# Attention in a fused block: divisions in whole steps, narrow diagonal steps unsummed, the bias earlier, another order at the end

## The chip, the cores and the metric

The kernel runs on one core of one Trainium2 chip. The time is the device time of one execution in microseconds; the figure compared is the median of several runs. The core's engines work side by side, each on its own queue: TensorE (PE, with its weight loads listed as PEld), VectorE (DVE), ScalarE (ACT), GpSimd (POOL) and SyncE (SP, which here issues the transfers).

## What is computed

A block of a transformer on 2048 tokens of width 512: half a feed-forward layer, causal attention with 16 heads of 32, half a feed-forward layer again, each on a layer norm and each added to the residual.

```python
x = x + 0.5 * _L0_ffn_ref(_layernorm(x, axis=-1), ...)
x = x + _L0_attn_ref(_layernorm(x, axis=-1), ...)
x = x + 0.5 * _L0_ffn_ref(_layernorm(x, axis=-1), ...)

# _L0_attn_ref
qkv = jnp.einsum('bsd,ed->bse', x, w_qkv) + b_qkv
...
scores = jnp.einsum('bhqd,bhkd->bhqk', q, k) / math.sqrt(Hd)
causal = jnp.triu(jnp.full((S, S), -jnp.inf, dtype=scores.dtype), k=1)
attn = jax.nn.softmax(scores + causal[None, None], axis=-1)
out = jnp.einsum('bhqk,bhkd->bhqd', attn, v)
...
return jnp.einsum('bsd,ed->bse', out, w_out) + b_out
```

All is float32. The feed-forward layers also unpack 4-bit weights; the change does not touch them.

## The kernel before

The program is one hand-ordered stream: the order in which the Python code calls the operations is the order of each engine's queue. Three stages follow each other: the first feed-forward layer, attention, the second feed-forward layer.

Attention takes the heads two at a time, in eight pairs `p`. Within a pair the 2048 queries are four blocks `g` of 512. `attend` walks over the key tiles (128 keys each) of a block, in an order in which the four tiles on the diagonal stand last (blocks 0 to 2) or in the middle (block 3). So a pair has 4 + 8 + 12 + 16 = 40 steps. In one step PE makes the scores of one key tile for both heads of the pair (lines 1323 and 1332, transposed: keys in the partitions, queries along the free axis), ACT takes the exponential into a tile `pt` (line 1357), and two steps later PE multiplies it with the values (line 1255). In the diagonal steps only the queries from the offset `off` on (0, 128, 256 or 384) are alive; the 128x128 corner of one head is masked by DVE on the scores, that of the other by ACT's copy (1350), a select on POOL (1351) and ACT's exponential (1359). In the same steps PE and DVE work ahead: `maxima(p + 1)` makes the scores of the next pair once more the other way round (line 1183), and DVE takes their largest values (1191, 1195), which come back as a negative row through `split` (1201 to 1220) and are added to the scores by PE in line 1323. Pair 0's maxima are made before any `attend`, in a loop of 40 steps.

The softmax denominators come from PE too: a matmul of line 1255 with a tile of ones in place of the values. To halve their number, two neighbouring steps' exponentials are first added up (`add`, lines 1378 and 1380): by POOL in pairs 0 to 6, by DVE in pair 7. If the second step's offset is larger, the first step's remaining columns are copied (line 1378). The sum of a diagonal pair is made at the end of the step after it. Only the last two steps of block 3 are left unsummed, with two matmuls in place of one. `columns` puts the 512 queries of two heads into four groups of 32 output partitions: the even and odd 128-query parts of each head.

At the end of a block, ACT copies numerators and denominators out of the bank (`both`, line 1277). In pairs 0 to 6 the denominators go through memory into a packed form, are inverted there (line 1289, four steps later), and come back spread out as `rc`; from the eighth step on, POOL multiplies (`chunk`, line 1301), one 32x128 piece for each head and each 128 queries, two at a step. Pair 7 inverts directly (line 1298). `at` sets the step at which such a piece is put into the stream.

After every second pair, `project_out` multiplies the finished 128 rows with the output weights and DVE adds the result to the residual tiles `xs` (line 1139); pair 7's share is in `o2` and `o3`. The output bias is added to `xs` by POOL in the first 16 steps of pair 0 (line 1487). The scores, maxima and projections share seven PSUM banks (`ps_one`).

At the end of attention stand: the transposed, normed tokens `xT_f` for the second feed-forward layer; sums of their blocks (`outer_sums`, `inner_first`); the last values matmuls; pair 7's last divisions; and 12 output projections. The second feed-forward layer begins by sending residual tiles 8 to 15 to memory (line 657), on SP's queue ahead of the weight loads, and with further sums on DVE (lines 695 and after).

Of the kernel before, what the change touches and what calls it, by code (L numbers as in the profile page):

```python
# [10 lines left out]
F32 = mybir.dt.float32  # L11
# [5 lines left out]
ALU = mybir.AluOpType  # L17
AX = mybir.AxisListType

P = 128  # L20
# [3 lines left out]
HD = 32  # L24
NT = S // P
NB = S // 512
NG = 8
NPAIR = H // 2
# [7 lines left out]
def macaron_kernel(ctx: ExitStack, tc: tile.TileContext, x, packed, scales, wqk, bqk, wv, bv, wo, bo, out):  # L36
# [6 lines left out]
    nc = tc.nc  # L43
# [18 lines left out]
    xs = [xpair[t // 2][:, t % 2, :] for t in range(NT)]  # L62
# [978 lines left out]
    def attention(xT, xT_f, wqk_wv, next_w):  # L1041
        with tc.tile_pool(name="aw", bufs=1) as aw, tc.tile_pool(name="qk", bufs=1) as qkp, tc.tile_pool(
            name="pp", bufs=4
# [87 lines left out]
            def project_out(u):  # L1131


                def piece(t):
                    po = ps_one.tile([P, 512], F32, tag="one", name=f"pp_{u}_{t}")
                    nc.tensor.matmul(  # L1136
                        po, lhsT=attnT[u][:, bass.ts(t, P)], rhs=wo_sb[:, u, :], start=True, stop=True
                    )
                    nc.vector.tensor_tensor(xs[t], po, xs[t], ALU.add)

                return [lambda t=t: piece(t) for t in range(NT)]

            def quadrant(p, a):
                r = 2 * (p % 2) + a
                return slice(HD * r, HD * r + HD)
# [4 lines left out]
            def at(steps, piece):  # L1150
                divisions.setdefault(now + steps, []).append(piece)
# [77 lines left out]
            def attend(p, width):  # L1229
# [7 lines left out]
                def order(g):  # L1237
                    return around(g, list(range(4 * g)), list(range(4 * g, 4 * g + 4)))
# [27 lines left out]
                def values(g, n, off, pt):  # L1266
                    c = order(g)[n]
                    if n == 0:

                        avs[0] = ps_acc.tile([P, 2, 256], F32, tag="acc", name=f"av_{p}_{g}")  # L1270
                    columns(0, pt, off, v=vals[:, c, p % 4, :], start=(n == 0))
                    last = n + 1 == len(order(g))
                    if (n > 0 and n % 2 == 0) or last:
                        denominators()
                    if last:
                        both = an.tile([P, 2, 256], F32, tag="both", name=f"both_{p}_{g}")
                        nc.scalar.copy(both, avs[0])  # L1277
                        rc = dens[g % 2]
                        direct = p == NPAIR - 1
                        if not direct:  # L1280

                            flat = store.tile([4, 256], F32, tag=f"flat{g % 2}", name=f"flat_{p}_{g}")
                            packs = an.tile([16, 64], F32, tag="packs", name=f"packs_{p}_{g}")
                            for r in range(4):
                                nc.sync.dma_start(out=flat[r : r + 1, :], in_=both[HD * r : HD * r + 1, 1, :])
                            nc.sync.dma_start(out=packs, in_=flat.rearrange("a (j n) -> (a j) n", j=4))

                        def inverse():
                            nc.vector.reciprocal(packs, packs)
                            back = store.tile([4, 256], F32, tag=f"back{g % 2}", name=f"back_{p}_{g}")  # L1290
                            nc.sync.dma_start(out=back.rearrange("a (j n) -> (a j) n", j=4), in_=packs)
                            for r in range(4):
                                nc.sync.dma_start(out=rc[HD * r : HD * r + HD, :], in_=back[r].partition_broadcast(HD))

                        def chunk(j):
                            n = slice(j // 2 * P, j // 2 * P + P)
                            if direct and j % 2 == 0:
                                nc.vector.reciprocal(rc[:, n], both[:, 1, n])
                            for a in range(2):
                                r = slice(HD * (2 * a + j % 2), HD * (2 * a + j % 2) + HD)  # L1300
                                nc.gpsimd.tensor_tensor(
                                    dst[quadrant(p, a), bass.ts(4 * g + j, P)], both[r, 0, n], rc[r, n], ALU.mult
                                )

                        if not direct:
                            at(4, inverse)
                        for j in range(4):
                            at((2 if direct else 8) + j, lambda j=j: chunk(j))

                def step(g, n, copied):  # L1310
                    c = order(g)[n]
# [51 lines left out]
                    def tail():  # L1363
                        while summing:
                            summing.pop(0)()
                        if n % 2 == 1:
                            (one, off_1), (other, off_2) = two
                            two.clear()
                            if g + 1 == NB and n + 1 == len(order(g)):

                                summed.append([(one, off_1), (other, off_2)])
                            else:
                                s = pp.tile([P, 2, 512], F32, tag="sum", name=f"sum_{p}_{g}_{n}", bufs=2)
                                eng = nc.vector if p + 1 == NPAIR else nc.gpsimd

                                def add():
                                    if off_1 < off_2:
                                        eng.tensor_copy(s[:, :, off_1:off_2], one[:, :, off_1:off_2])
                                    for a in range(2):
                                        eng.tensor_tensor(s[:, a, off_2:], one[:, a, off_2:], other[:, a, off_2:], ALU.add)  # L1380

                                summed.append([(s, off_1)])

                                if off_2:
                                    summing.append(add)
                                else:
                                    add()
                        if len(pending) > 2:
                            pending.pop(0)()
# [17 lines left out]
            def block_of(n):  # L1407
                return max(g for g in range(NB) if STARTS[g] <= n)
# [21 lines left out]
            for n, (matmuls, rest, diagonal) in enumerate(maxima(0)):  # L1430
                for a in range(2):
                    matmuls(a)
                for a in range(2):
                    rest(a, now)
                now += 1
                run_later(now)
                for step in norms[:2]:
                    step()
                del norms[:2]
                if n >= 4 and (n - STARTS[block_of(n)]) % (block_of(n) + 1) == 0:  # L1440
                    fill.pop(0)()
            assert not fill
# [10 lines left out]
            for p in range(NPAIR):  # L1453
# [29 lines left out]
                for steps in attend(p, 2 if p + 1 == NPAIR else 1):  # L1483
                    if n in STARTS:
                        fill = [fills[STARTS.index(n)], 4]
                    if p == 0 and n < NT:
                        nc.gpsimd.tensor_tensor(xs[n], xs[n], bo_sb, ALU.add)
                    other = next(ahead, None)
                    for a in range(2):
                        for maxrows, *_ in steps:  # L1490
                            maxrows(a)
                        if other:
                            other[0](a)
                    for a in range(2):
                        for _, matmuls, *_ in steps:
                            matmuls(a)
                    if other:
                        other[1](0, now)
                    for _, _, rest, _, _ in steps:
                        rest()  # L1500
                    if other:
                        other[1](1, now)
                    for _, _, _, tail, _ in steps:
                        tail()
                    for *_, diagonal in steps:
                        after_step(diagonal, fill)
                        for step in extra.get(n, ()):
                            step()
                        n += 1
            assert not later  # L1510

            xT_f += [x_transposed("f2_sums", tb) for tb in (2, 3)]
            for step in outer_sums(*xT_f, nc.vector) + inner_first(xT_f[0], xT_f[3]):
                step()
            while pending:
                pending.pop(0)()
            rest = o2[12:] + o3[8:12]
            for piece in rest[:4]:
                piece()
            for when in sorted(divisions):  # L1520
                for step in divisions[when]:
                    step()
            for piece in rest[4:] + o3[12:]:
                piece()

    xT_a, xT_f, early = [], [], {}
# [106 lines left out]
```

## Time and profile before

| what | us |
|---|---|
| median of 3 runs (3196.23 to 3198.35) | 3198.1 |
| the profiled execution | 3200.64 |
| its span, first to last instruction | 3198.9 |

The profile is one execution, recorded instruction by instruction. In the lines quoted later a group names its line, engine, operation, what it writes and reads, the shape and the count; in a timeline the first two numbers are start and duration in us, and a bracket gives the idle time before and what ended it. One matmul of the program gives two records[...]. Busy times by stretch of attention (borders set by the eye, near the pairs' borders):

| stretch, us | what | length | PE busy | DVE | ACT | POOL |
|---|---|---|---|---|---|---|
| 1193 to 1287 | projections, maxima of pair 0 | 94 | 93.11 | 54.98 | 17.75 | 5.65 |
| 1287 to 1407 | pair 0 | 120 | 113.07 | 62.13 | 54.16 | 81.47 |
| 1407 to 1492 | pair 1 | 85 | 80.72 | 52.38 | 47.74 | 64.28 |
| 1492 to 1599 | pair 2 | 107 | 103.27 | 55.91 | 50.07 | 64.08 |
| 1599 to 1699 | pair 3 | 100 | 99.98 | 64.18 | 47.75 | 64.44 |
| 1699 to 1820 | pair 4 | 121 | 121.00 | 59.22 | 50.40 | 64.05 |
| 1820 to 1911 | pair 5 | 91 | 90.98 | 63.27 | 49.05 | 64.63 |
| 1911 to 1993 | pair 6 | 82 | 77.58 | 50.15 | 48.08 | 64.08 |
| 1993 to 2071 | pair 7 | 78 | 73.18 | 57.66 | 45.66 | 26.55 |
| 2071 to 2090 | tail | 19 | 16.33 | 18.43 | 1.98 | 3.61 |

Length less busy time is how long an engine stood. The pairs differ in length because pairs 0, 2, 3, 4 and 5 also carry projections in their diagonal steps.

### The profile page before, as it was taken

The page shows a single profiled execution, that of the slowest core. Times are in us where ns is not written, and L with a number is a line of the kernel's source. Part 1 is how long each engine was busy: PE and PEld are TensorE (multiplying, and loading weights), DVE is VectorE, ACT ScalarE, POOL GpSimd, SP SyncE. Part 2 cuts the span into 40 slices and gives each one's busy share as a digit, 9 for nine tenths or more (in the row PEclk, how much of TensorE's full clock was granted, in tenths as well). Part 3 has the DMA queues.
Part 4 walks back from the last instruction along what each step waited for, and adds up shares of the span by engine and source line. Part 5 has one row for each costly group of instructions (what it writes and reads, how often), then busy time and mean ns, then how long its engine had stood idle before and what let it go on. Part 6 is the DMA issues. An engine that isn't in the chain of part 4 may idle for free.

```text
span 3198.9 us, 45147 instructions
## 1 busy us (share of the span) xinstructions
PE 3127.4 (98%) x16464; PEld 2006.0 (63%) x16464; DVE 2061.4 (64%) x3209; ACT 1048.0 (33%) x2070; POOL 1577.4 (49%) x1710
## 2 busy tenths in 40 slices
PE   7999999999999999999999999999999989999998
PEld 3556565656556575333335433478888878888887
DVE  6666666666666655565564566777666766766675
ACT  5111111111111121355453455533333333333332
POOL 3767584756767660676674577323232222223222
PEclk9999999999999999999999999999999999999999
DMA  4223222212223210000000000064444435444441
GB/s 138 81 84 115 86 76 82 96 60 96 78 84 116 79 63 7 5 14 9 12 9 7 28 20 9 3 192 136 124 126 129 122 122 165 122 123 128 126 125 60
DMA packets 261293, 260.21 MB, mean 81 GB/s; under 512 B 21216, under 2 KB 225616, under 8 KB 257104
## 3 DMA queue, kind: packets, MB, share of 16 engines
q1 hardware_dynamic: 261072, 257.33, 24.7%
q8 instruction: 130, 2.13, 0.3%
q14 instruction: 91, 0.75, 0.1%
HBM read 176.28 MB, written 79.92 MB: 80 GB/s over the span
## 4 chain that ended last, share of the span: by engine, by line
PE 91%; POOL 3%; DVE 2%; ACT 1%; issue 1%; DMA 1%; SPq 0%; POOLq 0%; ACTq 0%; DVEq 0%
PE d_f L737 12%; PE po L438 12%; PE pu L339 12%; PE pg L339 11%; PE pod_f L866 7%; PE av L1255 6%; PE f_f L737 6%; PE pm L1183 6%; PE pof_f L866 3%; PE pqk L1099 3%; PE e_f L737 3%; PE ps L1323 2%; PE pv L1116 2%; PE poe_f L866 2%; PE pp L1136 2%; PE ps L1332 1%
## 5 line engine op out<-in xcount | busy, mean ns | idle before, releaser
L1195 DVE TENSOR_REDUCE parts<-pm 128x1 f32<-128x512 f32 x384 | 246.6, 686 | 159.5 <-PE pm L1183 159.1
L1357 ACT ACTIVATE pt<-ps 128x512 f32<-128x512 f32 (+3 forms) x608 | 288.0, 528 | 179.2 <-PE ps L1332 132.1
L1183 PE MATMUL pm<-kT,qT 32*128 32x512 f32 (+3 forms) x1280 | 335.5, 579 | 0.2
L737 PE MATMUL d_f<-ys_f,ring 128*128 128x256 f32 x1216 | 321.2, 385 | 8.7 <-DVE o_f L770 8.7
L1380 POOL TENSOR_TENSOR sum<-pt,pt 128x512 f32<-128x512 f32 (+2 forms) x266 | 271.3, 1042 | 66.3 <-ACT pt L1357 64.4
L1332 PE MATMUL ps<-qT,kT 32*128 32x512 f32 (+3 forms) x1280 | 281.5, 540 | 0.0
L737 PEld LDWEIGHTS d_f<-ys_f,ring 128*128 128x128 f32 x1216 | 227.7, 191 | 55.9 <-DVE o_f L770 23.5
L438 PEld LDWEIGHTS po<-wd,inter 128*128 128x128 f32 x1024 | 194.4, 190 | 77.5 <-issue 56.0
L791 DVE TENSOR_TENSOR o_f<-o_f,o_f 128x1024 f32<-128x1024 f32 x128 | 203.6, 1601 | 58.2 <-ACT o_f L776 54.4
L438 PE MATMUL po<-wd,inter 128*128 128x256 f32 x1024 | 241.1, 379 | 0.0
L339 PE MATMUL pg<-xT_f,w 128*128 128x512 f32 x512 | 238.9, 594 | 1.4 <-ACT u L378 1.4
L339 PE MATMUL pu<-xT_f,w 128*128 128x512 f32 x512 | 238.0, 592 | 0.0
L881 POOL TENSOR_TENSOR xq<-xq,d_f 128x512 f32<-128x512 f32 x48 | 64.8, 1351 | 293.8 <-DVE xq L875 228.3
L452 POOL TENSOR_TENSOR xq<-xq,d 128x512 f32<-128x512 f32 x124 | 161.6, 1314 | 92.0 <-DVE xq L446 55.8
L791 POOL TENSOR_TENSOR o_f<-o_f,o_f 128x1024 f32<-128x1024 f32 x48 | 128.7, 2682 | 142.7 <-ACT o_f L776 141.5
L881 POOL TENSOR_TENSOR xq_second<-xq_second,d_f 128x512 f32<-128x512 f32 x45 | 61.4, 1365 | 273.2 <-DVE xq_second L875 218.8
L1255 PE MATMUL av<-pt,vals 128*32 128x256 f32 (+1 forms) x2432 | 190.1, 370 | 0.5 <-ACT both L1277 0.4
L393 POOL TENSOR_TENSOR u<-u,u 128x512 f32<-128x512 f32 x64 | 81.9, 1279 | 210.1 <-ACT u L390 210.1
L438 PEld LDWEIGHTS po<-wd,s 128*128 128x128 f32 x768 | 145.5, 190 | 57.9 <-issue 39.7
L438 PE MATMUL po<-wd,s 128*128 128x256 f32 x768 | 181.4, 379 | 0.0
L339 PE MATMUL pg<-xsum,w 128*128 128x512 f32 x384 | 178.8, 595 | 0.0
L339 PE MATMUL pu<-xsum,w 128*128 128x512 f32 x384 | 177.7, 592 | 0.0
(222 smaller groups left out, 6389.0 us busy)
## 6 DMA issues: line engine op xcount, KB each, us to landing
wd_f<-kept SPq DMA_DIRECT2D x112, 256.0 KB
kept<-wd SPq DMA_DIRECT2D x8, 1792.0 KB
xq<-in_x SPq DMA_DIRECT2D x16, 256.0 KB
pk<-in_gate_codes SPq DMA_DIRECT2D x16, 256.0 KB
sc<-in_gate_scales SPq DMA_DIRECT2D x32, 128.0 KB
pk<-in_up_codes SPq DMA_DIRECT2D x16, 256.0 KB
sc<-in_up_scales SPq DMA_DIRECT2D x32, 128.0 KB
pk<-in_down_codes SPq DMA_DIRECT2D x16, 256.0 KB
```

What stands on the lines that cost most here:

```text
L339: nc.tensor.matmul(ps, lhsT=a[:, j, :], rhs=b[:, j, :], start=(j == 0), stop=(j == 1))
L438: nc.tensor.matmul(ps[:, j, :], lhsT=a[i][:, k, bass.ts(2 * q + j, P)], rhs=b[i][:, k, :], start=(k == 0), stop=(k == 1),)
L452: adder.tensor_tensor(dst, dst, other, ALU.add)
L737: nc.tensor.matmul(ps[:, k, :], lhsT=fa[k][y], rhs=fb[k][y], start=first and k == 0, stop=True, skip_group_check=True,)
L791: sums.append(lambda: eng.tensor_tensor(dst, dst, other, ALU.add))
L866: nc.tensor.matmul(ps[:, j, :], lhsT=a[:, k, bass.ts(2 * q + j, P)], rhs=wd[:, PLACE[i], k, :], start=new and j == k == 0, stop=True, skip ...
L1183: nc.tensor.matmul(ps[a][:, :n], lhsT=q[r, bass.ts(4 * g + i, P)], rhs=k[r, kb * 512 : kb * 512 + n], start=True, stop=True,)
L1195: nc.vector.tensor_reduce(most, scores, AX.X, ALU.max)
L1255: nc.tensor.matmul(dst_, lhsT=lhsT, rhs=rhs, start=kw.get("start", False), stop=True, skip_group_check=True)
L1332: nc.tensor.matmul(ps[a][:, off:], lhsT=k[r, bass.ts(c, P)], rhs=q[r, g * 512 + off : (g + 1) * 512], start=False, stop=True,)
L1357: nc.scalar.activation(pt[:, a, plain[a] :], ps[a][:, plain[a] :], AF.Exp, scale=scale)
L1380: eng.tensor_tensor(s[:, a, off_2:], one[:, a, off_2:], other[:, a, off_2:], ALU.add)
```

## The change

Five things are done. The narrow second pair of diagonal steps (`off_1 == 2 * P`) of every block, and the last pair of every block, are no longer summed: their denominators come from both exponential tiles. In pairs 0 to 6 the division is made in four POOL operations of 32 x (2 x 128) where there were eight of 32 x 128, each taking one head's even or odd parts, at other steps, set for each block by `when`. In pair 7 the sum of the first head stays on DVE and that of the second goes to POOL. The bias is added in steps 12 to 27 of the loop of pair 0's maxima. At the end, one of the four `outer_sums` goes to POOL, the divisions are put ahead of the projections and of the other sums, and every other one of the first eight projections is copied from its bank by ACT and added by POOL; the four that follow stay on DVE.

```diff
-                def piece(t):
+                def piece(t, copy=None):
                     po = ps_one.tile([P, 512], F32, tag="one", name=f"pp_{u}_{t}")
...
-                    nc.vector.tensor_tensor(xs[t], po, xs[t], ALU.add)
+                    if copy is None:
+                        nc.vector.tensor_tensor(xs[t], po, xs[t], ALU.add)
+                    else:
+
+                        nc.scalar.copy(copy, po)
+                        nc.gpsimd.tensor_tensor(xs[t], copy, xs[t], ALU.add)
...
                         def chunk(j):
                             n = slice(j // 2 * P, j // 2 * P + P)
-                            if direct and j % 2 == 0:
+                            if j % 2 == 0:
                                 nc.vector.reciprocal(rc[:, n], both[:, 1, n])
...
-                        if not direct:
+                        def divided(a, h):
+                            r = slice(HD * (2 * a + h), HD * (2 * a + h) + HD)
+                            to = dst[quadrant(p, a), bass.ts(g, 512)].rearrange("p (x y n) -> p x y n", x=2, y=2)[:, :, h, :]
+                            x_, y_ = [v.rearrange("p (x n) -> p x n", x=2) for v in (both[r, 0, :], rc[r, :])]
+                            nc.gpsimd.tensor_tensor(to, x_, y_, ALU.mult)
+
+                        if direct:
+                            for j in range(4):
+                                at(2 + j, lambda j=j: chunk(j))
+                        else:
+
                             at(4, inverse)
-                        for j in range(4):
-                            at((2 if direct else 8) + j, lambda j=j: chunk(j))
+                            when = ((9, 10, 11, 12), (12, 13, 14, 15), (9, 10, 11, 12), (10, 10, 11, 11))[g]
+                            for k in range(4):
+                                at(when[k], lambda k=k: divided(k // 2, k % 2))
...
-                            if g + 1 == NB and n + 1 == len(order(g)):
+                            if n + 1 == len(order(g)) or off_1 == 2 * P:
 
                                 summed.append([(one, off_1), (other, off_2)])
                             else:
                                 s = pp.tile([P, 2, 512], F32, tag="sum", name=f"sum_{p}_{g}_{n}", bufs=2)
-                                eng = nc.vector if p + 1 == NPAIR else nc.gpsimd
+
+                                engines = (nc.vector if p + 1 == NPAIR else nc.gpsimd, nc.gpsimd)
 
                                 def add():
                                     if off_1 < off_2:
-                                        eng.tensor_copy(s[:, :, off_1:off_2], one[:, :, off_1:off_2])
-                                    for a in range(2):
+                                        engines[0].tensor_copy(s[:, :, off_1:off_2], one[:, :, off_1:off_2])
+                                    for a, eng in enumerate(engines):
                                         eng.tensor_tensor(s[:, a, off_2:], one[:, a, off_2:], other[:, a, off_2:], ALU.add)
...
+                if 12 <= n < 12 + NT:
+                    nc.gpsimd.tensor_tensor(xs[n - 12], xs[n - 12], bo_sb, ALU.add)
...
-                    if p == 0 and n < NT:
-                        nc.gpsimd.tensor_tensor(xs[n], xs[n], bo_sb, ALU.add)
...
             xT_f += [x_transposed("f2_sums", tb) for tb in (2, 3)]
-            for step in outer_sums(*xT_f, nc.vector) + inner_first(xT_f[0], xT_f[3]):
+            t3, t2, t4, t1 = outer_sums(*xT_f, nc.vector)
+            for step in (t3, t2, outer_sums(*xT_f, nc.gpsimd)[3]):
                 step()
             while pending:
                 pending.pop(0)()
-            rest = o2[12:] + o3[8:12]
-            for piece in rest[:4]:
-                piece()
             for when in sorted(divisions):
                 for step in divisions[when]:
                     step()
-            for piece in rest[4:] + o3[12:]:
+            for step in [t4] + inner_first(xT_f[0], xT_f[3]):
+                step()
+            spare = [pp.tile([P, 2, 512], F32, tag="pt", name=f"spare_{i}") for i in range(2)]
+            for i, piece in enumerate(o2[12:] + o3[8:12]):
+                if i % 2:
+                    piece(spare[i // 4][:, i // 2 % 2, :])
+                else:
+                    piece()
+            for piece in o3[12:]:
                 piece()
```

More of the change, by code (lines that the diff above doesn't have):

```diff
@@ L1138, in piece @@
                     )
-                    nc.vector.tensor_tensor(xs[t], po, xs[t], ALU.add)
-                return [lambda t=t: piece(t) for t in range(NT)]
+                    if copy is None:
[3 more added lines that the diff above has]
+                        nc.gpsimd.tensor_tensor(xs[t], copy, xs[t], ALU.add)
+                return [lambda *args, t=t: piece(t, *args) for t in range(NT)]
             def quadrant(p, a):
```

## The prediction

> **What bounds the kernel now.** I read the page's totals first, then the busy time by stretch (the table above), then what TensorE waited for inside attention, then the timelines around those waits. The totals say that only TensorE (PE) matters as a whole:
>
> ```profile
> PE 3127.4 (98%) x16464; PEld 2006.0 (63%) x16464; DVE 2061.4 (64%) x3209; ACT 1048.0 (33%) x2070; POOL 1577.4 (49%) x1710
> ```
>
> So a saving on another engine counts only where PE waits for it. The change touches attention alone (1193 to 2083 us) and its hand-over. In the table PE leaves 27.8 us of these 897 idle, in pairs 0, 1, 2, 6 and 7 and in the tail; in pairs 3 to 5 almost nothing. The view of waits, for PE in 1193 to 2110 us (total, times, longest), begins:
>
> ```profile
> PE av L1255 <- POOL sum L1378: 17.5, 9, 2.1
> PE pt_f L155 <- DVE xn_f L149: 2.1, 2, 1.8
> PE ps L1323 <- ACT pt L1357: 1.9, 3, 1.3
> ...
> PE pp L1136 <- POOL attnT L1301: 1.8, 1, 1.8
> PE av L1255 <- POOL sum L1380: 1.2, 2, 0.6
> ```
>
> One wait carries it: PE's denominator matmuls (line 1255) stand nine times before a sum whose first instruction is the copy of line 1378, that is before the sum of a narrow diagonal pair. Timelines of PE and POOL around the one in pair 1, block 1:
>
> ```profile
> 1427.09 0.41 PE L1255 MATMUL av<-pt,vals 128*32 128x128 f32 x4
> 1429.47 1.23 PE L1255 MATMUL av<-sum,ones_f 128*32 128x128 f32 x8 [1.96 <-POOL sum L1378]
> 1430.63 0.41 PE L1219 MATMUL row<-identb,split 128*64 128x128 bf16 x4
> ...
> 1423.34 1.96 POOL L1380 TENSOR_TENSOR sum<-pt,pt 128x384 f32<-128x384 f32 x2
> 1425.25 0.97 POOL L1301 TENSOR_TENSOR attnT<-both,den 32x128 f32<-32x128 f32 x2
> 1426.29 0.29 POOL L1351 TENSOR_SCALAR_AFFINE_SELECT pt<-pt 128x128 f32<-128x128 f32 x1
> ...
> 1427.98 0.97 POOL L1301 TENSOR_TENSOR attnT<-both,den 32x128 f32<-32x128 f32 x2
> 1429.02 0.40 POOL L1378 COPY sum<-pt 128x256 f32<-128x256 f32 x1
> 1429.37 0.87 POOL L1380 TENSOR_TENSOR sum<-pt,pt 128x128 f32<-128x128 f32 x2
> ```
>
> The narrow sum needs 1.27 us, but it starts at 1429.02, behind a wide sum, two divisions and five small steps. PE had its last values matmul at 1427.09 and gets on at 1430.63: 3.54 us. The same place in pair 4, where project pieces give POOL time:
>
> ```profile
> 1716.34 0.28 PE L1255 MATMUL av<-pt,vals 128*32 128x128 f32 x2
> 1716.35 0.48 PE L1255 MATMUL av<-sum,ones_f 128*32 128x128 f32 x6
> 1716.76 0.41 PE L1219 MATMUL row<-identb,split 128*64 128x128 bf16 x4
> ```
>
> There, counted the same way, it is 0.43 us. The nine are, read alike: pair 0 3.62, 3.58, 3.37; pair 1 3.54, 3.91; pair 2 3.50, 3.37; pair 6 3.68, 3.54: together 32.1 us. Four more (pairs 3 and 5, blocks 1 and 2) took 1.12 to 1.39, together 5.0.
>
> [...]a ready sum stood behind divisions nobody waited for. [...]here 128x512 takes 1272 ns and 128x128 456, so (1272-456)/384 = 2.1 ns. [...]eight records in four column groups need 0.43 us above. [...]One DVE add of 128x1024 takes 1.23 alone, and with POOL beside it:
>
> ```profile
> 2092.74 1.23 DVE L791 TENSOR_TENSOR o_f<-o_f 128x1024 f32<-128x1024 f32 x1
> ...
> 2105.83 4.53 DVE L791 TENSOR_TENSOR o_f<-o_f,o_f 128x1024 f32<-128x1024 f32 x2 [1.10 <-ACT o_f L776]
> 2105.88 3.40 POOL L791 TENSOR_TENSOR o_f<-o_f,o_f 128x1024 f32<-128x1024 f32 x1 [3.01 <-ACT o_f L776]
> ```
>
> **Part 1: narrow pairs unsummed.** The last pair of blocks 0 to 2 and the second diagonal pair of block 3, 32 in all, lose their sum: POOL loses 28 x (0.40 + 2 x 0.456) = 36.7 us. The ones-matmul now reads the exponentials themselves, which the values matmul just before it reads too, so no new wait arises. PE pays for it: 4 + 2 matmuls in place of 4. The second tile's two fall on the two column groups that the values matmuls also use: a third pass of 0.43/2 = 0.21 us. The place should thus take 0.64 us, stalled or not. The nine: 32.1 - 9 x 0.64 = 26.3. The four: 5.0 - 2.6 = 2.4. Of the other 11, pairs 1, 2 and 6 at block 0 took 0.67, 0.82, 0.67 (about +0.2 in all); eight took 0.43: -1.7. The eight in block 3 cost -1.7. Sum 25.5.
>
> **Part 2: divisions.** 28 blocks go from 8 POOL products of 32x128 (463 ns) to 4 of 32x256. No row has that form; slope 2.1 gives 463 + 128 x 2.1 = 735 ns; bounds 463 (no growth) and 926 (twice the old one). So 28 x (3.70 - 2.94) = 21 us of POOL. Their due steps matter more: block 1's move out of block 2's diagonal. But block 3's go to steps 10 and 11 of the next pair's block 1, so two (1.47) stand before the last masking select (line 1351) where one (0.97) stood; ScalarE's exponential of that tile comes 0.5 us later, and in pair 1 it ended (1426.93) only 0.16 us before its reader started (1427.09). I charge 0.5 in pairs 1 to 6: -3.0. The readers of these products, the output projections, come a pair later.
>
> **Part 3: bias.** 16 POOL adds of 1.27 us leave pair 0's steps for steps 12 to 27 of the first maxima, where POOL is busy 5.65 of 94 us. They only have the five split instructions (1.1 us) queued behind them, used three steps later. Cost 0; without that cover at most one 1.27. Gain: the two waits for line 1380 are in pair 0, 1.2.
>
> **Part 4: pair 7's sums shared.** DVE keeps 15 adds and 4 copies of 38 and 8; POOL gets 15 adds of about 1.2 us. A sum is used some two double steps later, so 1.27 on POOL against 1.29 for two on DVE changes nothing by itself. PE waited 4.8 us in pair 7, mainly for DVE and ScalarE behind POOL's divisions; the relief could take 4, the select and the power step behind a POOL add[...] could add 3. I take 0.
>
> **Part 5: the end.** Before, DVE works without a hole from 2068.93 to 2084.31, where the second feed-forward's sums (line 695) begin:
>
> ```profile
> 2074.93 2.48 DVE L1139 TENSOR_TENSOR xq<-pp,xq 128x512 f32<-128x512 f32 x4
> 2077.33 1.75 DVE L1298 RECIPROCAL den<-both 128x128 f32<-128x128 f32 x2
> 2079.00 4.36 DVE L1139 TENSOR_TENSOR xq<-pp,xq 128x512 f32<-128x512 f32 x7
> ...
> 2078.41 4.07 POOL L1301 TENSOR_TENSOR attnT<-both,den 32x128 f32<-32x128 f32 x8 [15.82 <-DVE den L1298]
> ```
>
> DVE loses one 128x1024 difference (1.22) and four adds (2.5): 3.7 us at best. Against it: POOL takes that difference (2.4 us, line 791's fastest), then 8 products (4.1), then four adds (1.27 each, after four ScalarE copies of 0.59, on an idle engine). [...]serially POOL ends its products near 2080 and its second add near 2082.8, for which DVE's last add (tile 15) waits, to 2083.5. That leaves 0.8. POOL's last two adds then meet line 695's work, up to 2 us more, and the copy of tiles 8 to 11 to memory, first in SP's queue before the weight fetches, waits for them too (2081.4 before, up to 2085 after). Bounds +3.7 and -1.2; I take +1.3, their middle.
>
> **Sum.** 25.5 - 3.0 + 1.2 + 0 + 1.3 = 25.0 us. The profiled execution took 3200.6 (span 3198.9), 2.5 above the median; less 25.0 it would be 3175.6, and the median 3198.1 becomes 3173.
>
> **Rivals.**
> - ScalarE takes over the wait. In the trace the held exponential leaves four more (2.04 us) queued at each diagonal's end while PE stands; without the stop PE would reach the score banks (seven) before they are free. For: at 1426.84 these four run just when PE stops. Against: in pair 0 the select gets 1.2 us earlier. 1.3 us at nine places, 12 us: 3185.
> - [...]DVE's relief is real: 2.4 more in the tail, 4 in pair 7, and the 3.0 not charged: 3164.
> - Slower: the last masking select decides. If POOL's queue still delays the last diagonal exponential by the 2 us that PE now waits, the values matmul waits for it in place of the sum. Its place is steps 10 to 11 of each block, its price all of part 1's gain, with the extra passes of 32 x 0.21 = 6.7 us left: 3205. It decides from about 2.2 us more queue before the select, where I count 0.5, and the 0.16 us of slack in pair 1 speaks for it.
>
> **Chances.** A measurement of this kernel tells 0.2%, 6.4 us, from no change. Forecast 0.66, ScalarE 0.16, full relief 0.14, slower 0.04. The ends of parts 2, 4 and 5 spread the forecast by some 8 us either way; with both faster rivals the range is 3162 to 3188. Faster 0.94, same 0.03, slower 0.03 (the last case lies at the bound and is split).
>
> **What would show it.** Right: no wait of PE for a narrow sum; PE waits in attention down from 27.8 to under 8 us; pair 1 near 80 us for 85, pairs 3 to 5 unchanged within 1. Wrong: a row of waits of PE for the exponentials (lines 1357 or 1359 of before) of over 5 us; line 695's first operation later after the last `both` copy than now (13.7 us); wide division products over 926 ns.

## The result, and the profile after

| | us | ratio to before |
|---|---|---|
| before, median of 4 runs (3195.88 to 3198.35) | 3197.16 | |
| after, median of 4 runs (3162.54 to 3171.1) | 3167.05 | 0.9906, 95% interval 0.9888 to 0.9923 |
| after, the profiled execution | 3169.56 | its span 3167.8 |

The change takes 30 us away; 25 were forecast. The runs of after lie 8.6 us apart, and they follow the mean clock granted to TensorE: 3162.54 and 3164.53 us at 0.997, 3169.56 at 0.994, 3171.1 at 0.993. Single microseconds between versions are therefore no finding here. Stages of one execution can be compared more closely, as long as it is known where the clock was low in them.

The totals line of the page after, to be laid beside that of before:

```profile
PE 3117.8 (98%) x16592; PEld 2010.6 (63%) x16592; DVE 2050.2 (65%) x3177; ACT 1047.8 (33%) x2074; POOL 1546.1 (49%) x1534
```

PE executes 128 matmul records more than before (64 matmuls of two records each, two for each of the 32 unsummed pairs; before, line 1332 left 1280 records for 640 matmuls in float32, line 1323 640 for 640 in bf16) and is still busy 10 us less: the nine stops of before took 32.1 us together, and only 17.5 of them count as idle in the trace. POOL has 176 instructions fewer. The view of waits for PE in attention (1193 to 2080 us; total, times, longest), with line numbers of after, which are up to 17 higher in attention:

```profile
PE d_f L737 <- ACT u_f L754: 2.7, 1, 2.7
PE pt_f L155 <- DVE xn_f L149: 2.3, 2, 2.1
PE av L1260 <- ACT both L1282: 2.3, 5, 0.6
PE ps L1339 <- ACT pt L1373: 1.2, 1, 1.2
PE d_f L737 <- DVE o_f L770: 1.0, 1, 1.0
PE pt_a L155 <- ACT xn_a L146: 0.6, 1, 0.6
```

The first row of before (17.5 us, nine times, for the sum of a narrow pair) is gone without a successor of its size. One row grew: PE waits for the copy `both` (0.4 before). One is new: PE waits once, for 2.7 us, at the first step of the second feed-forward layer.

How far each pair moved, read from the trace as the time between the copies `both` that end block 3 of successive pairs (pair 0 from the first projection):

| pair | 0 | 1 | 2 | 3 | 4 | 5 | 6 | 7 | last `both` to the first op of line 791 |
|---|---|---|---|---|---|---|---|---|---|
| before | 213.71 | 85.42 | 106.84 | 100.76 | 121.73 | 90.05 | 81.15 | 77.92 | 22.11 |
| after | 205.19 | 79.39 | 101.30 | 100.05 | 121.95 | 89.32 | 74.42 | 77.61 | 22.87 |
| difference | -8.52 | -6.03 | -5.54 | -0.71 | +0.22 | -0.73 | -6.73 | -0.31 | +0.76 |

The pairs give 28.4 us and the hand-over takes 0.8 back. Part of these differences is the clock: before, a stretch of 3.4 us at half clock (granted clock 0.51 by the view) lies in each of the pairs 0, 1, 2 and 6; after, there is one of 6.8 in pair 0 (0.51), one of 3.4 in pair 7 (0.53) and one of 3.4 in the hand-over (0.53). The span shrank by 31.1: the other 3.5 lie outside of attention, 3.0 of them in the second feed-forward layer from line 791 on, which the change doesn't touch. That part took 1106.1 us before and 1103.1 after, and between 1101.0 and 1105.5 in the traces of the kernels below, so the 3.0 are put down to scatter.

Here is the place of the prediction's second quotation, pair 1 at the end of block 1, in the timelines of POOL, ACT and PE after:

```profile
1414.27 1.95 POOL L1397 TENSOR_TENSOR sum<-pt,pt 128x384 f32<-128x384 f32 x2
1416.17 1.51 POOL L1314 TENSOR_TENSOR attnT<-both,den 32x256 f32<-32x256 f32 x2
1417.76 0.29 POOL L1367 TENSOR_SCALAR_AFFINE_SELECT pt<-pt 128x128 f32<-128x128 f32 x1
...
1419.44 1.51 POOL L1314 TENSOR_TENSOR attnT<-both,den 32x256 f32<-32x256 f32 x2
...
1418.08 0.31 ACT L1375 ACTIVATE pt<-pt 128x128 f32<-128x128 f32 x1 [2.81 <-POOL pt L1367]
1418.30 2.04 ACT L1373 ACTIVATE pt<-ps 128x512 f32<-128x512 f32 x4
1420.98 0.58 ACT L1282 COPY both<-av 128x512 f32<-128x512 f32 x1 [0.65 <-POOL attnT L1314]
...
1418.07 0.67 PE L1260 MATMUL av<-pt,vals 128*32 128x128 f32 x3
...
1418.58 0.27 PE L1260 MATMUL av<-pt,vals 128*32 128x128 f32 x1
1418.59 0.70 PE L1260 MATMUL av<-pt,ones_f 128*32 128x128 f32 x9
1419.41 0.41 PE L1224 MATMUL row<-identb,split 128*64 128x128 bf16 x4
...
1421.62 0.64 PE L1260 MATMUL av<-pt,vals 128*32 128x256 f32 x8 [0.61 <-ACT both L1282]
```

Three things are to be seen. The last step's values matmuls begin at 1418.07, and `row` follows at 1419.41: 1.35 us by the unrounded times, where it took 3.54. It would take 0.78, as most block ends now do, but the select on POOL comes 3.49 us after the start of the wide sum ahead of it (2.95 before), since two wide products now stand before it; the second head's exponential ends at 1418.39, and PE's values matmul for it (1418.45) stands within a group of records that counts as busy. And at this place there is a new wait: the copy `both` needs a buffer that the last products of the pair before still read, so it stands 0.65 us for POOL (line 1314), and PE 0.61 for the copy.

The hand-over after, timelines of DVE, POOL, ACT and PE:

```profile
2047.50 3.07 DVE L1140 TENSOR_TENSOR xq<-pp,xq 128x512 f32<-128x512 f32 x5
2051.85 1.92 DVE L1140 TENSOR_TENSOR xq<-pp,xq 128x512 f32<-128x512 f32 x3 [1.28 <-POOL xq L1144]
2053.68 1.13 DVE L695 TENSOR_TENSOR ys_f<-xT_f_sums,xT_f 128x512 f32<-128x512 f32 x1
2054.85 1.63 DVE L696 TENSOR_TENSOR ys_f<-xT_f,ys_f 128x512 f32<-128x512 f32 x1
...
2041.39 3.39 POOL L624 TENSOR_TENSOR xT_f<-xT_f,xT_f 128x1024 f32<-128x1024 f32 x1 [3.98 <-DVE xT_f_sums L621]
2044.85 5.62 POOL L1306 TENSOR_TENSOR attnT<-both,den 32x128 f32<-32x128 f32 x8
2050.55 5.38 POOL L1144 TENSOR_TENSOR xq<-spare,xq 128x512 f32<-128x512 f32 x4
...
2055.97 0.58 ACT L754 COPY u_f<-d_f 128x512 f32<-128x512 f32 x1 [6.56 <-POOL xq L1144]
...
2056.60 2.07 PE L737 MATMUL d_f<-ys_f,ring 128*128 128x256 f32 x4 [2.66 <-ACT u_f L754]
```

DVE waits 1.28 us for the first of POOL's four adds (the second then ends just in time), and line 695 begins 11.9 us after the last `both` (13.7 before). But ACT's first copy of the next layer (`u_f`) waits until POOL's fourth add has ended, and PE waits for that copy.

### The profile page after: what moved, and what is told of

It is laid out like the page before. It is cut to its first block, busy times and chain, and to the rows that moved or that the text cites. A ratio compares the mean times of both kernels' runs of the same rounds, so it can differ in the third digit from the quotient of the medians.

```text
span 3167.8 us, 45167 instructions
## 1 busy us (share of the span) xinstructions
PE 3117.8 (98%) x16592; PEld 2010.6 (63%) x16592; DVE 2050.2 (65%) x3177; ACT 1047.8 (33%) x2074; POOL 1546.1 (49%) x1534
## 5 line engine op out<-in xcount | busy, mean ns | idle before, releaser
L1397 POOL TENSOR_TENSOR sum<-pt,pt 128x512 f32<-128x512 f32 (+1 forms) x225 | 265.5, 1200 | 91.7 <-ACT pt L1373 89.5
```

## The experiments

Each kernel is compared with before, in runs on the same chip; a single run has no interval. All line numbers in profiles are those of the kernel in question.

**The unsummed pairs alone, and everything else.** Before with the one condition of after, and after with the condition of before:

```diff
-                            if g + 1 == NB and n + 1 == len(order(g)):
+                            if n + 1 == len(order(g)) or off_1 == 2 * P:
```

> The kernel before, with the narrow pairs unsummed and nothing else. My theory (TensorE's long waits are for narrow sums that stand late in GpSimd's queue, so taking the sums away takes the waits away, whatever else is in that queue): 22 to 25 us less than before, the waits for the copy of line 1378 gone, 0.64 us at each block's end. Rival 1 (the backlog of GpSimd is the cause, and the waits pass on to the exponential held by the last masking select): 8 to 14 us less, with new waits of TensorE for lines 1357 or 1359. Rival 2 (the gain comes from the other parts): 0 to 7 us more than before.

> The changed kernel with the narrow pairs summed as before. My theory: most of the gain is lost; only where the moved divisions and bias no longer stand ahead of a narrow sum is the wait shorter (pair 0, and block 2 of pairs 1, 2 and 6), so 11 to 17 us less than before, 14 to 20 more than the changed kernel. Rival 1 (backlog: any relief of GpSimd does it): 25 us or more less than before. Rival 2 (the sums alone matter): within 4 us of before.

The first took 3173.54 us (0.9924, interval 0.991 to 0.9939), 23.4 less than before; the second 3182.98 (0.9951, 0.9934 to 0.9968), 14.0 less. Both lie in the range that the theory gave. The rival, that PE's stops came from POOL's backlog as such and that any relief would take them away (25 us or more from the second kernel), falls; so does the one that the waits would pass on to the exponentials. In the waits of PE in the first kernel (1193 to 2100 us) the row of the narrow sums is gone and that of the exponentials as before:

```profile
PE av L1255 <- POOL sum L1380: 2.8, 4, 1.7
PE ps L1323 <- ACT pt L1357: 1.9, 3, 1.3
```

Pair 1, block 1 of the second kernel, POOL and then PE:

```profile
1414.78 0.29 POOL L1367 TENSOR_SCALAR_AFFINE_SELECT pt<-pt 128x128 f32<-128x128 f32 x1
...
1416.46 1.51 POOL L1314 TENSOR_TENSOR attnT<-both,den 32x256 f32<-32x256 f32 x2
1418.04 0.40 POOL L1395 COPY sum<-pt 128x256 f32<-128x256 f32 x1
...
1418.49 1.46 PE L1260 MATMUL av<-sum,ones_f 128*32 128x128 f32 x8 [2.61 <-POOL sum L1395]
```

With the wide divisions and still the sum, PE stands longer than before (2.61 us for 1.96), because now 1.51 us of products lie between the small steps and the sum (0.97 before), and as much more ahead of the select. In pairs 1, 2 and 6 the end of block 1 takes 4.7 to 4.8 us here, against 3.5 to 3.7. The divisions' new steps are good only once nobody waits for a sum there. The gains of the two kernels add up to 37.4 us, the whole change brought 30: some stops were open to either cure. In pair 0 and at the ends of block 2 relief of POOL was enough (0.93 to 1.23 us in the second kernel, with the sum in place).

**The bias alone.**

```diff
+                if 12 <= n < 12 + NT:
+                    nc.gpsimd.tensor_tensor(xs[n - 12], xs[n - 12], bo_sb, ALU.add)
...
-                    if p == 0 and n < NT:
-                        nc.gpsimd.tensor_tensor(xs[n], xs[n], bo_sb, ALU.add)
```

> The kernel before, with the bias added in the loop of the first maxima and nothing else. My theory: only pair 0 gets shorter, each of its three waits by the 1.27 us of one bias addition, and the two short waits for line 1380 go: 4 to 6 us less. Rival (the additions ran beside TensorE anyway): within 1.5 us of before in pair 0's stretch. A third way: the loop of the first maxima gets longer, by up to 1.3 us.

3191.11 us (0.998, 0.9972 to 0.9988), 5.8 less, as expected. Pair 0 falls from 213.71 to 206.64, the others stay within 0.4. The ends of pair 0's blocks 0 to 2, 3.62, 3.58 and 3.37 us before, took 0.94, 1.10 and 3.57, where each was to lose 1.27: without the bias adds in POOL's queue, two of pair 0's three stops go even with the sum in place.

**The divisions alone** (before with `divided` and its steps `when`, as in the diff above).

> The kernel before, with the divisions in fewer pieces and at the other steps, and nothing else. My theory: block 2 of pairs 0, 1, 2 and 6 loses about 2 us each (two divisions of 0.97 no longer ahead of the narrow sum), block 1 of pairs 1, 2 and 6 gains nothing or loses 0.5: 6 to 8 us less in all, and one product of 32x256 takes 735 ns (463 to 926). Rival 1 (fewer instructions relieve GpSimd everywhere): 12 us or more. Rival 2 (no effect, or block 1 loses more than block 2 gains): 0 to 3 us more.

3189.81 us (0.9976, 0.9966 to 0.9986), 7.1 less, as expected in all. A 32x256 product took 0.724 us on average. The stops at the ends of block 2 go, but those of block 1 in pairs 1, 2 and 6 grow to between 4.55 and 4.89 us, as in the second kernel: by 1.0 to 1.2 us, where at most 0.5 was expected. Those of pairs 3 and 5 grow from 1.25 to 2.30.

**Pair 7's sums shared, alone.**

```diff
-                                eng = nc.vector if p + 1 == NPAIR else nc.gpsimd
+                                engines = (nc.vector if p + 1 == NPAIR else nc.gpsimd, nc.gpsimd)
```

> The kernel before, with pair 7's sums shared between DVE and GpSimd and nothing else. Read from the trace: the stretch between the last block copies of pair 6 and pair 7, 77.9 us before. My theory: within 1 us of it. Rival 1 (DVE's relief counts): 74 to 76. Rival 2 ([...]selects stand behind sums): 79.5 to 81. The narrow sums stay in this kernel, half of each on GpSimd.

One run took 3200.07 us against 3197.47, and pair 7 took 80.71 instead of 77.92. The expectation is missed, and what had been named as its rival is there, in the timelines of POOL, ACT and PE:

```profile
2004.55 2.98 POOL L1301 TENSOR_TENSOR attnT<-both,den 32x128 f32<-32x128 f32 x6
2007.61 0.29 POOL L1351 TENSOR_SCALAR_AFFINE_SELECT pt<-pt 128x128 f32<-128x128 f32 x1
...
2007.93 0.31 ACT L1359 ACTIVATE pt<-pt 128x128 f32<-128x128 f32 x1 [2.58 <-POOL pt L1351]
...
2008.84 0.21 PE L1323 MATMUL ps<-wo_bo,ones_b 3*128 3x128 bf16 x1 [2.37 <-ACT pt L1357]
```

The select stands behind divisions that POOL's new sums have pushed back, ACT stands for the select, and PE for a score bank that ACT has not emptied. PE's waits between 1993 and 2071 us come to 5.4 us in the view, 4.6 before in the same stretch; what made up the rest of the 2.8 us was not shown. In after, where POOL has less to do, PE's longest wait of this kind in pair 7 is 1.19 us, and the pair takes 77.61.

**The end alone** (before with after's `piece` and its last section).

> The kernel before, with the end in the new order and nothing else. From the trace: the time from the last block copy (both) to the first sum o_f of two outputs in the second feed-forward layer, 22.1 us before, 22.9 in the changed kernel. Theory formed on that trace (ScalarE's first copy of the second layer writes to memory that attention's pools held, and so waits for GpSimd's last addition): 22.5 to 23.3, with the wait of ScalarE for line 1144's counterpart, and line 695's first sum 1.5 to 2 us earlier than before. Rival (the loss in the changed kernel comes from pair 7 or from DVE's own queue): 21.0 to 22.2.

One run took 3198.74 us against 3197.47. Line 695 begins 11.91 us after the last `both`, as expected, and the first operation of line 791 at 21.74, a gain of 0.4 where a loss of that size or more was expected. ACT's copy and PE:

```profile
2086.40 0.59 ACT L754 COPY u_f<-d_f 128x512 f32<-128x512 f32 x1 [6.58 <-POOL xq L1144]
...
2087.04 1.13 PE L737 MATMUL d_f<-ys_f,ring 128*128 128x256 f32 x4 [2.68 <-ACT u_f L754]
```

The wait is the same as in after (2.68 and 2.66 us). What differs is the clock behind it. The view by stretch, first after, then this kernel (borders, length, busy time of PE, PEld, DVE, ACT, POOL with instructions, granted clock, DMA share, GB/s):

```profile
2056.50:2060.00 3.50, 3.40 (x9) 2.77 (x10) 2.57 (x4) 1.12 (x3) 0.00 (x0) 0.55 0.95 391
```

```profile
2087.00:2090.50 3.50, 3.46 (x16) 2.88 (x16) 3.43 (x6) 1.06 (x2) 0.00 (x0) 1.00 0.99 405
```

In 3.5 us PE has 9 records at clock 0.55 and 16 at 1.00. The second kernel of the experiments (everything but the unsummed pairs), which has the same end and the same wait (2.7 us), has line 791 at 22.82; its clock behind the wait was not shown.

**What holds `u_f`, and later divisions.** Two versions of after. Both put block 3's divisions one step later; the first also gives all additions of the end back to DVE, the second keeps POOL's adds but copies into tiles of `wo_bo` that are free by then, not into new `pt` buffers:

```diff
-                            when = ((9, 10, 11, 12), (12, 13, 14, 15), (9, 10, 11, 12), (10, 10, 11, 11))[g]
+                            when = ((9, 10, 11, 12), (12, 13, 14, 15), (9, 10, 11, 12), (11, 11, 12, 12))[g]
...
-                if i % 2:
-                    piece(spare[i // 4][:, i // 2 % 2, :])
-                else:
-                    piece()
+                piece()
```

```diff
-                    piece(spare[i // 4][:, i // 2 % 2, :])
+                    piece(wo_bo[:, bass.ts((0, 1, 4, 5)[i // 2], 512)])
```

> The changed kernel, with block 3's divisions one step later (11, 11, 12, 12 in place of 10, 10, 11, 11) and all projections of the end added by DVE again, in the new order. Theory: the block-1 waits of TensorE for the block copy (0.6 us in pairs 1, 2 and 6) go, pairs 1, 2 and 6 get shorter by 0.6 to 1.2 each; from the last copy to the first o_f 21.2 to 21.8 (22.9 in the changed kernel), though line 695 starts later (13.0 against 11.9). In all 2 to 5 us less than the changed kernel. Rival (the block copy waits for these divisions at whatever step they stand; the end is bound by DVE's count of additions): pairs 1, 2 and 6 unchanged or longer, o_f at 23 or later.

> The changed kernel, with block 3's divisions one step later as in the run beside it, and the copies of the end put into parts of the output weights' tile that are no longer read, which outlives attention's pools. Theory: ScalarE's first copy of the second layer no longer waits for GpSimd's additions; first o_f at 21.4 to 22.2 after the last copy, TensorE's wait for line 754 (2.7 us) gone, DVE's first sums (lines 695, 696) still slowed by GpSimd's additions. Rival (that wait is not what holds it): 22.7 or more.

They took 3166.40 us (0.9902, 0.9887 to 0.9917) and 3168.79 (0.9906, 0.989 to 0.9923): no difference from after can be told, and the 2 to 5 us expected of the first are missed. ACT's copy in the second:

```profile
2052.10 0.58 ACT L754 COPY u_f<-d_f 128x512 f32<-128x512 f32 x1 [3.83 <-DVE xq L1140]
```

It no longer waits for POOL's last add, though POOL makes the same four adds. So the memory was the link: attention's buffers, `spare` among them, are given up before those of the second layer, `u_f` among them, are made, and in after the copy into `u_f` waited 6.56 us for the last reader of `spare`. Line 791 begins 22.2 us after the last `both` here, since lines 695 and 696 still run beside POOL's adds (1.13 and 1.64 us) and PE then waits 3.0 us for DVE. With DVE alone (the first version) it is 21.3, the least seen, though line 695 starts a whole microsecond later than in after (12.9): it and line 696 then take 0.68 and 0.69 us. With the later divisions the ends of block 1 in pairs 1, 2 and 6 take 0.78 us (1.34 to 1.47 in after), so the select no longer holds them; but the wait for `both` grows from 0.6 to as much as 1.1, as the rival said, and the three pairs stay within 0.4 of what they were: one wait is exchanged for the other. The row in the waits of the first version (1193 to 2080 us):

```profile
PE av L1260 <- ACT both L1282: 3.5, 5, 1.1
```

**Earlier divisions, and a third buffer.** From the first of these two versions: the divisions at steps 8 to 10; the same with all of pair 7's sums on DVE; and, with the late divisions, three buffers for `both` (and for the norms' tiles, which share them):

```diff
-                            when = ((9, 10, 11, 12), (12, 13, 14, 15), (9, 10, 11, 12), (11, 11, 12, 12))[g]
+                            when = ((9, 10, 11, 12), (12, 13, 14, 15), (9, 10, 11, 12), (8, 9, 9, 10))[g]
```

```diff
-                                engines = (nc.vector if p + 1 == NPAIR else nc.gpsimd, nc.gpsimd)
+                                engines = (nc.vector if p + 1 == NPAIR else nc.gpsimd,) * 2
```

```diff
-                        both = an.tile([P, 2, 256], F32, tag="both", name=f"both_{p}_{g}")
+                        both = an.tile([P, 2, 256], F32, tag="both", name=f"both_{p}_{g}", bufs=3)
```

> The changed kernel, with block 3's divisions at steps 8, 9, 9, 10 (10, 10, 11, 11 there) and the projections of the end on DVE. Theory (at block 1 of pairs 1, 2 and 6 ScalarE's block copy waits for these divisions, because it writes over one of two buffers that they read; so they must be done earlier, not later): no wait of TensorE for the block copy over 0.25 us, pair 1 78.3 to 79.0, pair 2 100.0 to 100.7, pair 6 73.6 to 74.3 us; 2 to 6 us less than the changed kernel in all. Rival (they now stand before the masking selects of steps 9 to 11 and hold the exponentials back): new waits for line 1373 or 1375 of over 0.4 us each, pairs 1, 2 and 6 as in the changed kernel or longer.

> As the run beside it, with all sums of pair 7 on DVE as before the change. Read from pair 7's stretch (77.6 us in the changed kernel, 77.9 before). Theory: with the narrow sums gone and the divisions moved, sharing is worth nothing or up to 1 us: 77.5 to 79. Rival (sharing costs, as it did alone, 2.8 us): 74.5 to 76.5.

> The run with the divisions at 11, 11, 12, 12 and the end on DVE, with three buffers in place of two for the block copies. Theory (the copy waits for the divisions that read the buffer it writes): the waits of TensorE for the block copy, 0.97 to 1.13 us in pairs 1, 2 and 6, go to under 0.25. Rival (ScalarE is late for another reason, its four exponentials): they stay.

| | us | ratio and interval | pairs 1, 2, 6 | pair 7 |
|---|---|---|---|---|
| after | 3167.05 | 0.9906 (0.9888 to 0.9923) | 79.39, 101.30, 74.42 | 77.61 |
| early divisions | 3166.85 | 0.9900 (0.9883 to 0.9918) | 78.18, 100.14, 73.76 | 80.56 |
| early, pair 7's sums on DVE | 3165.76 | 0.9897 (0.9879 to 0.9915) | 78.18, 100.14, 73.76 | 78.16 |
| late, three buffers | 3164.2, one run | | 78.49, 100.14, 73.46 | 77.44 |

The view of waits of the last (PE, 1193 to 2080 us) still has the copy, at a sixth of after's total, as in before:

```profile
PE av L1260 <- ACT both L1282: 0.4, 2, 0.2
```

The early divisions end before both the select and the copy; with the late ones, the third buffer takes the copy's wait away. Either way pairs 1, 2 and 6 are 0.7 to 1.2 us shorter each: the buffer is the cause of what later divisions alone had left. The early divisions pay it back in pair 7, where POOL then has pair 6's products and half of the sums at once (PE waits 1.98 us for ACT, which waits for a select); with the sums on DVE that wait is 1.06 and the pair 2.4 us shorter. Only the 0.9 us of the wait are shown to come from the sharing; what made up the rest was not shown. The 78.16 us lie in the range expected; the reason given, that sharing is worth up to 1 us, is not borne out beside these divisions. The 2 to 6 us that were expected of the early divisions are in the pairs and not in the medians, whose intervals overlap with that of after. No version that clearly beats after was found.

## Why the prediction was right, and where it was not

The direction, the place and the main mechanism were right, and 3167.05 lies in the range. Step by step:

- **Part 1 (25.5 us).** Alone it gave 23.4 by the medians, and 25.5 in the pairs of its profiled execution, the fastest of its four. The block ends take 0.78 us wherever nothing else holds them, counted from the step's first values matmul; by the same count those without a stop took 0.56 before, so the two further matmuls cost 0.22, as worked out (0.21). (The 0.64 and 0.43 of the prediction were counted from a later record than the stops themselves, which makes the gain of the nine 1.3 us too high.) The match to a tenth is partly luck. In the trace of before, PE's clock was also halved for 3.4 us behind four of the stops (granted clock 0.51; an estimate: up to 1.7 us of work each, half of the 3.4), which the sum did not count, while this part's own execution had a granted clock of 1.00 in pair 0 (1193 to 1399.4 us) and a mean of 0.997 (0.993 before); on the other side, it left PE 2.3 us of waits for sums in pair 0, where the bias was still in POOL's queue.
- **Part 2 (charged 3.0).** This term had the wrong sign. The delay that was named is there: the select comes 0.54 us later, and the ends of block 1 in pairs 1, 2 and 6 take 0.56 to 0.69 us too long; pairs 3 to 5 don't feel it. The buffer of `both`, which was not named, costs 0.6 us more at each of the same three places, so the price of 3.0 (0.5 in each of six pairs) comes near the sum of the two in three pairs, 3.6, by chance. Against it stands what was valued at nothing: in pair 1, from the unsummed pairs alone to after, block 1 (between copies `both`) grows by 1.05 us, but block 2, whose diagonal no longer has divisions in the queue, shrinks by 1.34 and block 3 by 0.28. Pairs 1 to 6 together gained 0.7. The product's price (735 ns estimated from POOL's adds of line 1380, 724 measured) was right.
- **Part 3 (gain 1.2).** The cost of nothing holds: the view by stretch has POOL busy 25 us instead of 6 during pair 0's maxima, and no wait of PE for the five split instructions appears. The gain seems sized too small. Pair 0 takes 206.81 us with the unsummed pairs alone and 202.48 in the later versions, 4.3 us less (granted clock 1.00 in that stretch, both with the unsummed pairs alone and in the first of the later versions). Pair 0's own divisions have moved there too, and no run with the sums gone parts the two; alone, the bias gave 7.1 us in pair 0 (213.71 to 206.64) and the divisions 4.4 (to 209.32). For the bias, only the waits that the trace of before showed had been counted, not those that come up once the narrow sums are gone (1.7 us the longest). In the profiled after, 6.8 us at a granted clock of 0.51 hide most of this.
- **Part 4 (0, from -4 to +3, the author's estimates).** Pair 7 moved by -0.3, or -0.5 from the unsummed pairs alone to after. The price named (a select behind a POOL add or division) is there when the part stands alone: 2.8 us lost in one run, of which PE's waits in the view account for 0.8.
- **Part 5 (gain 1.3).** Line 695 starts 1.8 us earlier, within the bounds. DVE waits for POOL, though for its first add and not the second. But the step from there to PE failed: the copy `u_f` waits for POOL's last add through the memory, 2.66 us. The hand-over gains 0.4 us with a granted clock of 1.00 behind that wait (the end alone) and loses 0.8 with 0.55 (the profiled after).

The forecast 25.0 was 25.5 and -0.5 for all the rest. The medians say 23.4 and 6.7 (30.1 - 23.4). So the error lies in the small terms: by single traces, part 2 came out 3.7 and part 3 up to 3.1 us better than charged, part 5 and part 1 some 2 us worse each. That explains about half of the missing 5; the rest is within the scatter of the runs, and no run assigns it. The range was met, and the near match of the sum is in part errors that cancel.

The rival of full relief said 3164, and the time is nearer to that than to 3173, but not by its mechanism: the tail and pair 7 gave nothing like the 2.4 and 4 us that it needed; only the charge of part 2 was void. ScalarE did not take over the wait: PE's wait for exponentials is 1.2 us in all, 1.9 before. The last masking select did not decide either. PE's idle time in attention and the hand-over (1193 to 2061.5 us, the same stretch shifted by the pairs' gain) fell from 27.8 to 9.5 us, not under 8; without the wait for `u_f` it would be 6.8. Of the signs of a wrong theory none appeared: line 695 starts earlier, and the wide products stay under 926 ns on average.

## What to carry to other kernels

Where an engine stops for a small result, look at what stands ahead of the small operation in its queue. Not needing the result (here two extra matmuls, 0.22 us together at each place, on the busiest engine) was worth more than easing the producer's queue (23.4 us against 7.1 by the divisions and 5.8 by the bias). A wait that a trace shows can hide others (in pair 0 those for line 1380 took 1.2 us before, 2.3 with the narrow sums gone): with the first stop gone, ask which queue is late next, and which buffer the delayed work still holds, a stage later too. When moving work off an engine at a hand-over, see whether a later tile takes the memory that the moved work reads last (here PE stood 2.66 us for it).

## What the runs showed of the hardware

- **Behind some stops of about 2 us the granted clock was halved, behind others not.** Before, PE stood nine times for a narrow sum, between 1.79 and 2.09 us. Behind four of these stops (1.84, 2.09, 1.93 and 2.09 us, the ones that end at 1307.96, 1454.89, 1525.39 and 1934.94) the granted clock was 0.51 for 3.4 us; behind the other five (2.01, 1.79, 1.96, 1.79 and 1.97) it was 1.00. So the length of the stop alone doesn't tell. The same wait of 2.10 us in pair 7, first in after, then with three buffers; the timeline line, and the stretch behind it:

```profile
2022.07 1.13 PE L155 MATMUL pt_f<-ident,xn_f 128*128 128x128 f32 x4 [2.10 <-DVE xn_f L149]
```

```profile
2022.00:2025.50 3.50, 3.43 (x14) 1.73 (x18) 2.08 (x6) 2.14 (x8) 1.43 (x4) 0.52 0.00 0
```

```profile
2016.94 0.75 PE L155 MATMUL pt_f<-ident,xn_f 128*128 128x128 f32 x4 [2.10 <-DVE xn_f L149]
```

```profile
2018.00:2022.00 4.00, 3.23 (x38) 1.26 (x36) 2.80 (x9) 3.77 (x14) 0.79 (x3) 1.00 0.02 4
```

  Behind it the granted clock was 0.52 in after and 1.00 with three buffers. The wait for `u_f` differed likewise: 0.55 behind 2.66 us in after, 1.00 behind 2.68 us with the end alone. What decides was not shown. Each such stretch costs up to 1.7 us of PE's work (an estimate: half of the 3.4 us), about as much as the stop, and the places differ between the traces of before and after. The stretch in pair 0 of after (6.8 us at 0.51, from 1213.4 us) follows no wait over 0.6 us; what set that one off stays open.
- **POOL and DVE at once.** In after, POOL's 128x1024 difference took 3.39 us beside DVE (the median of line 791's on POOL was 2.36 before), and its eight 32x128 products 5.62 us (4.07 before). DVE's operations beside POOL's adds took longer as well: lines 695 and 696 took 1.13 and 1.63 us in after, and 0.68 and 0.69 without POOL (the first of the later versions).
